# Sorted experts: the first products of a group in two PSUM buffers, tile by tile in turn, instead of in the two banks of one

## The chip, the cores and the metric

The kernel runs on one core of one Trainium2 chip. The metric is the device time in microseconds (us). Engines are named as in the profile: PE is TensorE's matmuls and PEld its weight loads, DVE is VectorE, ACT is ScalarE, POOL is GpSimd, SP is SyncE. PSUM is the memory that matmuls write; its banks hold 512 fp32 values per partition.

## What is computed

The reference is a stack of blocks on 2048 tokens of 128 features (linear layers, attentions, feed-forward layers, experts). The part that the change touches is the last step of the block `L3_ffn`, which occurs twice in the stack, once before and once after the attention `L3_attn`. Every token picks its two best of eight experts by a gate; the larger of the two numbers is the expert that it is sent to. That expert is a product to 256 features, a normalization, a GELU and a product back to 128:

```
chosen = jnp.max(top_i, axis=-1)
def expert(W1, B1, G, Bt, W2, B2, rsc):
    hh = xr @ W1 + B1
    hh = jax.nn.gelu(_ln(hh, G, Bt), approximate=False)
    return (hh @ W2 + B2) * rsc + xr
...
outs = jax.vmap(expert)(w1, b1, ln_g, ln_b, w2, b2, res_scale)
sel = jnp.take_along_axis(outs.transpose(1, 0, 2), chosen[:, None, None], axis=1)[:, 0]
moe = sel * jnp.sum(wts, axis=-1, keepdims=True)
```

## The kernel before

The stages follow one another: layers 0, 1 and 2, then the attention of the gated block, its experts, the attention `rope3`, the second gated attention, and its experts again. The change lies in `Experts.run` (line 1363), which therefore runs twice.

The experts are sorted. `route` gives each token a place in a list of tiles of 128 tokens that all have the same expert; there are eight first tiles, one for each expert, and up to fifteen extra ones for experts with more than 128 tokens, 23 tiles in all whatever the routing. `run` first works out which token lies in which slot (`who`, line 1421). Then it takes the 23 tiles in groups of four, the last of three, so six groups. Each group goes through four functions:

- `turned(b)`, line 1440: for each tile, an indirect DMA of POOL's queue gathers 128 rows of tokens (`xt`, line 1451, a ring of 4 buffers), for an extra tile another one loads that expert's weights (`wt`, line 1458, a ring of 11 buffers), and PE transposes the rows into one PSUM bank (`g_tp`). ACT copies the group's four transposes to SBUF (`gT`, line 1464) and writes the expert's selector (`sel`, line 1443).
- `first_product(b)`, line 1467: for each tile, PE adds the bias by a 16-row matmul (`ph<-b_b1s,sel`) and the product by `wt` (`ph<-wt,gT`, two instructions) in a PSUM region of 128 x 256; DVE takes its statistics (`st`, `mv`). After the last tile, DVE makes the reciprocal roots (`rs`, eleven short instructions) and normalizes tile by tile out of PSUM into SBUF (`hn`).
- `turned_back(b)`, line 1487: PE transposes each `hn` in two halves (`h_tp`), ACT takes the GELU of each (`hT`, line 1498).
- `second_product(b)`, line 1503: per tile a bias matmul and four instructions by `wt` into one bank (`po`); DVE copies the group's result to SBUF (`og_s`), SP sends it to DRAM.

The loop at line 1523 sets the order: `turned(b + 1)`, `turned_back(b)`, `first_product(b + 1)`, `second_product(b)`. With `order["pinned"]` set, PE's matmuls and transposes keep exactly this order. The other engines' instructions in this stage are not pinned; the framework places them, and sets every semaphore. When all groups are done, indirect DMAs gather the results back to the tokens (`yg`, line 1538), and `tail(c)` adds them to `x`, followed by what comes behind the experts: `rope3.prepare(c)` in the first run, `store(c)` in the second.

PSUM is shared out in pools (lines 1659 to 1661): `tp`, three buffers of one bank; `sc`, two buffers of two banks (`[P, 2, CW]`, 512 values each); `av`, one buffer of one bank. In this stage `bank(...)` takes a buffer of `tp`, `banks("ph")` a whole one of `sc`, and `out_bank` the one of `av`. In attention the score tiles `sn` take buffers of `sc` in turn (line 1027): PE writes one while DVE reduces the other. In `first_product`, one buffer of `sc` holds all four tiles of a group: tiles 0 and 1 in its first bank, 2 and 3 in its second.

Of the kernel before, what the change touches and what calls it, by code (L numbers as in the profile page):

```python
# [43 lines left out]
def tile_macaron(ctx: ExitStack, tc: tile.TileContext, a: dict, out: bass.AP):  # L44
# [30 lines left out]
    def mm(dst, lhsT, rhs, start=True, stop=True):  # L75
        pin(nc.tensor.matmul(dst, lhsT=lhsT, rhs=rhs, start=start, stop=stop))  # L76
# [98 lines left out]
    def inv_sqrt(pool, var, shape, tag, on_pool=False):  # L175
        v = pool.tile(shape, F32, tag=tag + "_v", name=tag + "_v")
        vec.tensor_scalar_add(v, var, 1e-5)
        g = pool.tile(shape, I32, tag=tag + "_g", name=tag + "_g")
        vec.tensor_scalar(g, v.bitcast(I32), -0.5, float(0x5F3759DF), ALU.mult, ALU.add)
        r = pool.tile(shape, F32, tag=tag + "_r", name=tag + "_r")  # L180
        prev = g.bitcast(F32)
        for _ in range(3):
            h = pool.tile(shape, F32, tag=tag + "_h", name=tag + "_h")
            if on_pool:
                nc.gpsimd.tensor_tensor(h, prev, prev, ALU.mult)
                nc.gpsimd.tensor_tensor(h, h, v, ALU.mult)
                nc.gpsimd.tensor_scalar(h, h, -0.5, 1.5, ALU.mult, ALU.add)
                nc.gpsimd.tensor_tensor(r, h, prev, ALU.mult)
            else:
                vec.tensor_tensor(h, prev, prev, ALU.mult)  # L190
                vec.scalar_tensor_tensor(h, h, -0.5, v, ALU.mult, ALU.mult)
                vec.scalar_tensor_tensor(r, h, 1.5, prev, ALU.add, ALU.mult)
            prev = r
        return r
# [477 lines left out]
    def ring(name, tag="w", shape=(P, CW), bufs=10):  # L672
        pool = pools["keep" if tag == "xnT" else "ring"]
        return pool.tile(list(shape), F32, tag=tag, name=name, bufs=bufs)
# [11 lines left out]
    def banks(name):  # L686
        if order["mode"] in ("host", "fill"):
            return TwoBanks(name)
        return pools["sc"].tile([P, 2, CW], F32, tag="sc", name=name)
# [6 lines left out]
    def out_bank(name):  # L696
        return pools["av"].tile([P, CW], F32, tag="av", name=name)
# [582 lines left out]
    class Experts:  # L1280
        F = 256
# [81 lines left out]
        def run(self, carried, after):  # L1363
# [8 lines left out]
            F, FB, NX = self.F, self.FB, self.NX  # L1372
# [44 lines left out]
            ps = out_bank("who_ps")[:, 0:NX]  # L1417
# [49 lines left out]
            def first_product(b):  # L1467
                s0, n = groups[b]
                g = made[b]
                mv = sb.tile([P, TC, 2], F32, tag="mv", name="mv", bufs=2)  # L1470
                ps = banks("ph")
                ph = [ps[:, k // 2, k % 2 * F : (k % 2 + 1) * F] for k in range(n)]
                for k in range(n):
                    mm(ph[k], g["sel"][:, k, :], b_1, stop=False)
                    mm(ph[k], g["gT"][:, k * P : (k + 1) * P], g["wts"][k][:, 0:F], start=False)
                    st = sb.tile([P, 6], F32, tag="st", name="st", bufs=2)
                    vec.bn_stats(st, ph[k])
                    vec.bn_aggr(mv[:, k, :], st)
                rs = inv_sqrt(sb, mv[:, :n, 1], [P, n], "rs")
                pair = [ring("hn") for _ in range(2)]  # L1480
                g["hn"] = [pair[k // 2][:, k % 2 * F : (k % 2 + 1) * F] for k in range(n)]
                for k in range(n):
                    vec.tensor_scalar(
                        g["hn"][k], ph[k], mv[:, k, 0:1], rs[:, k : k + 1], ALU.subtract, ALU.mult
                    )
# [34 lines left out]
            order["pinned"] = True  # L1520
            turned(0)
            first_product(0)
            for b in range(len(groups)):
                more = b + 1 < len(groups)
                if more:
                    turned(b + 1)
                turned_back(b)
                if more:
                    first_product(b + 1)
                second_product(b)  # L1530
# [259 lines left out]
```

## Time and profile before

| what | us |
|---|---|
| median of 3 runs (4014.67 to 4025.18) | 4024.48 |
| the profiled execution | 4027.38 |
| its span, first to last instruction | 4025.6 |
| expert stage, first run: first `ph` to last `og_s` | 2375.69 to 2468.32 |
| expert stage, second run | 3894.43 to 3987.21 |
| PE busy in 2365 to 2470 (105 us), granted clock 0.58 | 83.9 |
| DVE, ACT, POOL busy in the same stretch | 40.3, 23.8, 33.2 |

The profile shows one execution, with times in us from the start of the span. A line of the timeline gives the start, the length, the engine, the line of the kernel, the operation with what it writes and reads, the number of instructions, and in brackets how long the engine had been idle before and what released it. A line of a helper stands for all that call it: 76 is every matmul by `mm`, 84 every instruction of DVE, 94 every transpose. Matmuls overlap in the pipeline, so the distance from one start to the next tells more than the length of one. PEclk is the TensorE clock that was granted, 1.00 or 0.50 at any moment.

### The profile page before, as it was taken

The page shows a single profiled execution, that of the slowest core. Times are in us where ns is not written, and L with a number is a line of the kernel's source. Part 1 is how long each engine was busy: PE and PEld are TensorE (multiplying, and loading weights), DVE is VectorE, ACT ScalarE, POOL GpSimd, SP SyncE. Part 2 cuts the span into 40 slices and gives each one's busy share as a digit, 9 for nine tenths or more (in the row PEclk, how much of TensorE's full clock was granted, in tenths as well). Part 3 has the DMA queues.
Part 4 walks back from the last instruction along what each step waited for, and adds up shares of the span by engine and source line. Part 5 has one row for each costly group of instructions (what it writes and reads, how often), then busy time and mean ns, then how long its engine had stood idle before and what let it go on. Part 6 is the DMA issues. An engine that isn't in the chain of part 4 may idle for free. (4 is left out here: it accounts for less than half of the span.)

```text
span 4025.6 us, 72321 instructions
## 1 busy us (share of the span) xinstructions
PE 3590.0 (89%) x29144; PEld 1707.2 (42%) x29144; DVE 3117.3 (77%) x5468; ACT 2396.2 (60%) x4556; POOL 293.3 (7%) x473
## 2 busy tenths in 40 slices
PE   8789899699999999999999966688989899999965
PEld 8556655333333333333333333334333433333333
DVE  2855344689898986799999844689998799999844
ACT  1222133268686877688888722255767688888732
POOL 2000012220000000000000023200000000000013
PEclk8889789889999999799999965678899899999965
DMA  2100001111000000000000022310000000000012
GB/s 69 27 1 1 1 6 37 46 36 33 12 20 10 13 25 22 14 28 10 7 10 5 7 59 71 97 54 15 10 25 26 17 28 9 9 7 7 7 50 67
DMA packets 66063, 100.55 MB, mean 25 GB/s; under 512 B 10800, under 2 KB 31008, under 8 KB 65472
## 3 DMA queue, kind: packets, MB, share of 16 engines
q1 hardware_dynamic: 55184, 70.41, 5.8%
q0 software_dynamic: 9200, 24.94, 2.4%
q8 instruction: 230, 3.77, 0.4%
q14 instruction: 105, 0.86, 0.1%
q10 hardware_dynamic: 1344, 0.57, 0.1%
HBM read 65.29 MB, written 29.52 MB: 24 GB/s over the span
## 5 line engine op out<-in xcount | busy, mean ns | idle before, releaser
L84 DVE TENSOR_REDUCE h_mx<-sn 128x2 f32<-128x1024 f32 (+1 forms) x1856 | 2202.2, 1197 | 142.6 <-PE sn L1030 120.9
L1087 ACT ACTIVATE pr<-st 128x512 f32<-128x512 f32 x3712 | 1972.3, 585 | 486.2 <-PE st L76 319.6
L76 PE MATMUL av<-pr,va 128*32 128x256 f32 x14592 | 1193.6, 399 | 10.8 <-ACT h_ot L1116 10.2
L76 PE MATMUL st<-qp,kp 64*128 64x512 f32 x3712 | 1012.6, 501 | 34.7 <-ACT pr L1087 31.7
L1030 PE MATMUL sn<-kp,qp 64*128 64x512 f32 (+3 forms) x3712 | 826.3, 418 | 82.4 <-DVE h_mx L84 66.9
L76 PEld LDWEIGHTS st<-qp,kp 64*128 64x128 f32 x3712 | 401.9, 188 | 822.3 <-ACT pr L1087 448.4
L76 PEld LDWEIGHTS av<-pr,va 128*32 128x32 f32 x14592 | 294.3, 109 | 666.9 <-issue 626.0
L1030 PEld LDWEIGHTS sn<-kp,qp 64*128 64x128 f32 x3712 | 395.1, 196 | 132.7 <-DVE h_mx L84 80.9
L614 ACT ACTIVATE hid<-h 128x512 f32<-128x512 f32 x128 | 76.3, 597 | 235.3 <-PE h L76 229.7
L84 DVE TENSOR_TENSOR hid<-hid,h 128x512 f32<-128x512 f32 x128 | 87.4, 687 | 114.2 <-PE h L76 102.2
L76 PEld LDWEIGHTS po<-w_l_w3T,hid 128*128 128x128 f32 x1024 | 126.1, 193 | 39.0 <-issue 28.0
L76 PE MATMUL po<-w_l_w3T,hid 128*128 128x128 f32 x1024 | 127.7, 277 | 5.5 <-DVE hid L84 5.5
L76 PE MATMUL h<-m_xc,w_l_w12T 128*128 128x512 f32 x256 | 127.9, 638 | 0.0
L1458 POOL DMA_INDIRECT wt<-in_b_wt,w_row_i x30 | 28.7, 958 | 1245.2 <-DVE slot_i L84 1199.5
L76 PE MATMUL h<-xnT,w_l_w12T 128*128 128x512 f32 x256 | 117.4, 601 | 0.4 <-DVE logits L594 0.4
L84 DVE BATCH_NORM_STATS2 st<-ph 128x6 f32<-128x256 f32 x46 | 19.9, 432 | 90.3 <-PE ph L76 65.4
L247 POOL TENSOR_TENSOR x<-x,w_b_n2b 128x512 f32<-128x512 f32 x8 | 10.2, 1270 | 1064.0 <-ACT rows L213 1064.0
L1059 ACT CAST h_mT<-mt_ps 8x512 fp32r<-8x512 f32 x64 | 36.9, 576 | 75.9 <-PE mt_ps L94 75.6
L94 PE MATMUL xn_tp<-ident,xn_t 128*128 128x128 f32 x64 | 20.0, 390 | 63.5 <-ACT xn_t L213 52.7
L84 DVE TENSOR_TENSOR st<-st,mask_kq 128x128 f32<-128x128 f32 x256 | 63.4, 291 | 16.9 <-PE st L76 16.2
L76 PEld LDWEIGHTS h<-m_xc,w_l_w12T 128*128 128x128 f32 x256 | 49.9, 205 | 50.8 <-issue 48.1
L213 ACT ACTIVATE xn_t<-x,ln_nb,ln_r 128x128 f32<-128x128 f32 x64 | 26.4, 481 | 69.9 <-DVE ln_nb L84 49.1
(421 smaller groups left out, 2910.2 us busy)
## 6 DMA issues: line engine op xcount, KB each, us to landing
qp<-dq SPq DMA_DIRECT2D x128, 136.0 KB
kp<-dk SPq DMA_DIRECT2D x162, 64.0 KB
dq<-hi SPq DMA_DIRECT2D x32, 256.0 KB
dq<-lo SPq DMA_DIRECT2D x32, 256.0 KB
wt<-in_b_wt SPq DMA_DIRECT2D x16, 258.0 KB
qp<-h_mT SPq DMA_DIRECT2D x240, 4.0 KB
cos<-in_l_cos POOLq DMA_DIRECT2D x12, 256.0 KB
sin<-in_l_sin POOLq DMA_DIRECT2D x12, 256.0 KB
```

The source lines that it names most:

```text
L76: pin(nc.tensor.matmul(dst, lhsT=lhsT, rhs=rhs, start=start, stop=stop))
L84: ins = method(*args, **kw)
L94: pin(nc.tensor.transpose(dst, src, ident))
L213: nc.scalar.activation(dst[:, t, :], src[:, t, :], AF.Identity, bias=nb[:, t : t + 1], scale=rstd[:, t : t + 1])
L247: nc.gpsimd.tensor_tensor(xs, xs, row.unsqueeze(1).to_broadcast([P, TC, D]), ALU.add)
L614: nc.scalar.activation(hid[:, hb, :], p_1, AF.Silu)
L1030: pin(nc.tensor.matmul(sc[:, j, :wd], lhsT=qp[r, p, t * P : (t + 1) * P], rhs=kp[r, 2 * g + p, kc * CW : kc * CW + wd], start=True, stop=True,
L1059: nc.scalar.copy(mT, pt)
L1087: nc.scalar.activation(pr[:, off:CW], sc[:, off:], AF.Exp, scale=A.scale)
L1458: nc.gpsimd.indirect_dma_start(wts[k], None, a["b3_wt"], bass.IndirectOffsetOnAxis(ap=w_row_i[:, s - E : s - E + 1], axis=0),)
```

## The change

Where a group took one two-bank buffer of the pool `sc`, it now takes both. Of each it uses the first bank alone: tiles 0 and 2 lie in the two halves of the first buffer's bank, tiles 1 and 3 in those of the second. The matmuls, the statistics and the normalization are the same instructions in the same program order, on other addresses.

```diff
                 mv = sb.tile([P, TC, 2], F32, tag="mv", name="mv", bufs=2)
-                ps = banks("ph")
-                ph = [ps[:, k // 2, k % 2 * F : (k % 2 + 1) * F] for k in range(n)]
+
+                ps = [banks("ph") for _ in range(2)]
+                ph = [ps[k % 2][:, 0, k // 2 * F : (k // 2 + 1) * F] for k in range(n)]
                 for k in range(n):
                     mm(ph[k], g["sel"][:, k, :], b_1, stop=False)
                     mm(ph[k], g["gT"][:, k * P : (k + 1) * P], g["wts"][k][:, 0:F], start=False)
```

## The prediction

> **What bounds the kernel now.** I read the page first (shares, the clock line, the costliest groups), then the chain that ended last inside the expert stage, then the timelines of PE, DVE and POOL there, then the granted clock in stretches of 3.41 us.
>
> ```profile
> PEclk8889789889999999799999965678899899999965
> ...
> L84 DVE BATCH_NORM_STATS2 st<-ph 128x6 f32<-128x256 f32 x46 | 19.9, 432 | 90.3 <-PE ph L76 65.4
> ```
>
> The change touches only the expert stage, which runs twice: from the first `ph` to the last `og_s` copy, 2375.69 to 2468.32 (92.6 us) and 3894.43 to 3987.21 (92.8 us). The clock line sags there to 0.6 and 0.5. The statistics of the first products, 46 of 0.43 us, wait for PE each time. The chain in the first run, columns start, length, what:
>
> ```profile
> 2377.69 0.44 DVE st L84
> 2378.18 1.74 PE ph L76 x3
> 2379.95 0.44 DVE st L84
> 2380.43 1.74 PE ph L76 x3
> 2382.20 0.44 DVE st L84
> ```
>
> PE and DVE take turns: three matmuls of a tile, its statistics, the next tile. The timeline of PE says the same of every tile but the first of a group, of the third as well, which lies in the other bank. So the wait hangs on the whole two-bank buffer, not on the bank. At half clock:
>
> ```profile
> 2380.94 1.22 PE L76 MATMUL ph<-wt,gT 128*128 128x256 f32 x2
> 2382.69 0.58 PE L76 MATMUL ph<-b_b1s,sel 16*128 16x256 f32 x1 [0.52 <-DVE st L84]
> 2383.20 1.22 PE L76 MATMUL ph<-wt,gT 128*128 128x256 f32 x2
> 2384.21 1.06 PE L94 MATMUL g_tp<-ident,xt 128*128 128x128 f32 x4
> ```
>
> and at full clock:
>
> ```profile
> 2409.67 0.38 PE L76 MATMUL ph<-b_b1s,sel 16*128 16x256 f32 x1 [0.53 <-DVE st L84]
> 2409.97 0.70 PE L76 MATMUL ph<-wt,gT 128*128 128x256 f32 x2
> 2410.71 0.43 DVE L84 BATCH_NORM_STATS2 st<-ph 128x6 f32<-128x256 f32 x1 [0.88 <-issue]
> ...
> 2411.20 0.38 PE L76 MATMUL ph<-b_b1s,sel 16*128 16x256 f32 x1 [0.53 <-DVE st L84]
> ...
> 2411.51 0.70 PE L76 MATMUL ph<-wt,gT 128*128 128x256 f32 x2
> ...
> 2412.14 0.32 PE L76 MATMUL po<-b_b2s,sel 16*128 16x128 f32 x1
> ```
>
> **What goes: the waits.** Half clock: tile to tile is 2.25 us (2380.43 to 2382.69). Unwaited, the bias matmul takes 0.51 (2382.69 to 2383.20) and the pair 1.01 (2383.20 to 2384.21, where the next work starts): 1.52. A wait costs 0.73. Full clock: 1.53 against 0.31 + 0.63 = 0.94, so 0.59. After the change tile 1 has a buffer of its own, and tile 2 shares one with tile 0, whose statistics started 0.74 after its pair (2409.97 to 2410.71) and are done 0.48 later, at 1.22; tile 2 comes 0.63 + 0.94 = 1.57 after that pair. It is covered by tile 1, with 0.35 to spare at full clock; without that cover two waits a group come back. Groups of 4, 4, 4, 4, 4 and 3 tiles have 17 waits a run; counting pitches in the timelines, 10 at half and 7 at full clock in either run. Sum: 20 x 0.73 + 14 x 0.59 = 14.6 + 8.3 = **22.9 us**.
>
> **What the two buffers cost.** Formerly a group took one buffer and left the other to its neighbour. Now it takes both, so the next group needs them back. But PE's order is fixed, and the transposes `h_tp` of a group, which need all its `hn`, the last reader of the buffers, stand ahead of the next group's `ph`. That wait is paid already: 0. No instruction and no DMA is added. On ACT, eight GELUs (2406.64 to 2409.54) lie under the next `ph`; four unwaited tiles at full clock last 3.8 us from 2406.59, still 0.8 more. On DVE a tile's two statistics need 0.65, under 0.94.
>
> **What is moved: the clock.** The granted clock steps in stretches of 3.41 us (PE busy with its instructions, then the clock):
>
> ```profile
> core 0: us, PE busy (x), PEclk, DMA share, GB/s
> 2399.15:2402.56 3.41, 3.41 (x13) 0.50 0.19 29
> 2402.56:2405.98 3.42, 3.42 (x16) 0.50 0.62 194
> 2405.98:2409.39 3.41, 2.64 (x12) 1.00 0.49 135
> 2409.39:2412.80 3.41, 2.61 (x10) 1.00 0.37 105
> 2412.80:2416.22 3.42, 3.42 (x13) 0.50 0.29 75
> ```
>
> A dense stretch with transposes lifts it, and then the waited `ph` tiles leave PE 2.4 to 2.7 us of work in a stretch, and it falls back, so `po` runs at half. Sorting the whole trace's stretches so: of 805 at full clock with 2.8 us or more of work, 799 were followed by full clock; with 2.2 to 2.8 only 38 of 57; and at half clock none with under 3.0 us was ever lifted. Without waits `ph` and `po` leave PE full, so I expect the clock to hold once it is up. At full clock a group is 4 x 0.94 = 3.8 (`ph`), 4 x 0.98 = 3.9 (`po`, 3930.97 to 3931.95), and transposes of 0.9 and 0.5 (1.71 and 0.85 at half, less 0.40 for each four: 0.66 for four at 2330.24 at full clock against 1.06): 9.1 us.
>
> Then POOL is late next. Its queue issues four row and four weight gathers in a group:
>
> ```profile
> 2405.12 0.95 POOL L1451 DMA_INDIRECT xt<-xg,who  x1 [0.82 <-PE g_tp L94]
> ...
> 2406.38 0.95 POOL L1451 DMA_INDIRECT xt<-xg,who  x1 [0.30 <-issue]
> ```
>
> 8 x 1.25 = 10.0 us, so the three groups with weight gathers cost 10.0 each, not 9.1. A run then is: to the first `h_tp`, 12.4 less 3 x 0.73: 10.2; to the second, 17.2 less 2.2: 15.0, still at half clock; three groups at 10.0: 30.0; `h_tp`, three `ph`, four `po` at full clock: 7.6; the last group, whose `hn` (4.3 us behind its last statistics) now outlasts `po` by 0.5: 0.5 + 1.2 + 2.9 + 0.7 = 5.3. Together 68.1 against 92.6: 24.5 a run. If the clock rises a group earlier, lifted by bare `ph` (no row shows such a stretch), `ph` and `po` give 4.6 more, 29 a run; if a row gather, which lands 3.9 us after its issue (2371.39 to 2375.28), is 1 us later in each cycle, 3 less. I take 25, **50 us** for both. The profiled execution took 4027.4 (span 4025.6 and 1.8 around it), which gives 3977; the median shown is 2.9 lower: 4024.5 - 50 = 3974.5, rounded to **3975**.
>
> A rule that speaks against this last part: the Trainium skill, "TensorE: Matmul & The Clock Gate", section "Part 4: PE-mode transpose", says that transposes do not count as PE work for the clock. The trace disagrees: the stretch at 2399.15, `po` alone and full, was not followed by full clock, while the one at 2402.56, with transposes of rows and of `hn` in it, was. The same page, section "HAM oscillation — how this bites in real kernels", tells of PSUM double-buffering that gave no further gain in a kernel whose loop had been put in order: by it the sum would be 0. Here the wait that goes stands in the chain itself.
>
> **Rivals.**
> - *Only the waits go.* The clock goes on falling, since POOL's late rows leave gaps in each group; 10 of the 42 full-clock stretches with 2.4 to 2.8 us of work were followed by half clock. Then 22.9: 4001.6. For it: the fall at 2412.80 came after a stretch with 2.61. Against it: `po` after a dense `ph` has no gap before the next gathers. If the page's rule on transposes held, this is also what would come out.
> - *The waits stay*, because two buffers of the pool are tracked as one: 4024. Against it: attention's score tiles `sn` lie in the same pool, and DVE reduces one (1.20 us each, 2202 us busy with 143 idle before them) while PE writes the next.
> - *Slower, by POOL's queue.* Only PE's order is pinned; POOL's is chosen anew. If the fourth row gather lands behind the next group's weight gathers, which wait for `po` (issues at 2413.54, 2415.09 and 2416.64), it goes out at about 2417.9 instead of 2410.14. Its transpose then waits 5.2 to 6.5 us (a 1.25 issue or two and 3.9 to land behind the last `po`) in three cycles of each run: 31 to 39 us, less 22.9: up to 4040. It decides from 3.8 us a cycle (22.9 / 6) on. For it: one weight gather stands between row gathers today. Against it: nothing in the diff reaches POOL.
>
> **How the numbers follow.** Clock holds, 3962 to 3987: 0.62. Waits alone or a clock that holds in part, 3987 to 4012: 0.23. More than 62 us (full clock from the first group on): 0.04. Within 0.3% (12 us, about what a measurement of this kernel can tell from no change): 0.06, the waits that stay and part gains eaten by POOL. Slower by more: 0.05. The range runs from the early rise (58 us, and some drift of attention's clock: the three runs lie 10.5 us apart) to the waits alone and a little less: 3962 to 4005, which leaves out about 0.2.
>
> **What would show it.** The changed kernel should have no `ph` waiting for `st`; tile pitches of 1.52 and 0.94; clock 1.00 from the second `h_tp` of a run to its last `po`; the stage 92.6 down to 65 to 70 us; `g_tp` waiting for `xt` from the third group on. I am wrong if the clock still alternates (about 4002), if `ph` waits elsewhere, or if rows are later than 4 us a cycle.

## The result, and the profile after

| what | before, us | after, us |
|---|---|---|
| median of 4 runs each | 4023.93 (4014.67 to 4025.18) | 3968.77 (3968.13 to 3970.36) |
| the profiled execution, its span | 4027.38, 4025.6 | 3968.13, 3966.3 |
| expert stage, first run | 92.62 | 66.49 (2374.26 to 2440.77) |
| expert stage, second run | 92.78 | 66.23 |
| time at half clock in the two runs of the stage | 75.6, 75.7 | 27.5, 26.8 |
| all that lies between the two runs of the stage | 1426.1 | 1422.4 |

The ratio is 0.987 (95%: 0.9856 to 0.9884): 55 us less. The two stages give 26.1 and 26.5, together 52.7. The rest lies ahead of, between and behind them, where nothing was changed and where executions differ by a few us anyway.

The clock line of the page of after; the two runs of the stage (slices 24 and 25, and the last two) now show 0.7, where they showed 0.6 and 0.5. The single 5 lies behind the first run:

```profile
PEclk8889789879999999799999977578989899999977
```

The view of the tile `st` in the stage's first run, for the kernel after (what it waited for, who waited for it, each with us and times):

```profile
its engine sat idle before it (us, times) until:
  PE ph L76: 27.1, 23
who waited for it (us, times):
  PEld ph L76: 2.3, 7
```

All 23 statistics still wait for their product. The other direction is gone: in the same view of before, PE's matmuls waited for `st` 13 times by name (6.8 us) and its weight loads as often (14.0); here only seven weight loads do, 2.3 us in all, under matmuls that are still running. The chain of waits, first run, after:

```profile
2386.79 6.64 PE ph L76 x12
2393.43 6.21 PE po L76 x20
...
2402.03 3.76 PE ph L76 x12
2405.78 3.58 PE po L76 x20
```

Where PE and DVE took turns, twelve `ph` now stand in one piece, followed by twenty `po`. PE's timeline, after, at half clock and then at full clock:

```profile
2376.15 0.58 PE L76 MATMUL ph<-b_b1s,sel 16*128 16x256 f32 x1
2376.66 1.22 PE L76 MATMUL ph<-wt,gT 128*128 128x256 f32 x2
2377.81 0.58 PE L76 MATMUL ph<-b_b1s,sel 16*128 16x256 f32 x1
...
2402.90 0.38 PE L76 MATMUL ph<-b_b1s,sel 16*128 16x256 f32 x1
2403.20 0.70 PE L76 MATMUL ph<-wt,gT 128*128 128x256 f32 x2
2403.84 0.38 PE L76 MATMUL ph<-b_b1s,sel 16*128 16x256 f32 x1
```

No bracket, so no idle time; the pitch is 1.66 (2376.15 to 2377.81) and 0.94 (2402.90 to 2403.84). The granted clock in stretches of 3.41 us, after (columns: PE, PEld, DVE, ACT and POOL busy with instructions, then the clock, the DMA share and GB/s):

```profile
2391.46:2394.87 3.41, 3.41 (x9) 2.00 (x8) 1.84 (x8) 0.00 (x0) 0.00 (x0) 0.50 0.00 0
2394.87:2398.29 3.42, 3.42 (x12) 2.69 (x11) 3.07 (x12) 0.00 (x0) 1.89 (x2) 0.50 0.27 77
2398.29:2401.70 3.41, 3.41 (x16) 3.29 (x17) 0.69 (x1) 1.21 (x2) 2.22 (x3) 0.50 0.66 185
2401.70:2405.12 3.42, 3.42 (x14) 1.74 (x12) 1.46 (x5) 2.90 (x8) 2.53 (x3) 1.00 0.36 104
2405.12:2408.53 3.41, 3.41 (x19) 2.50 (x18) 2.70 (x14) 0.00 (x0) 2.22 (x3) 1.00 0.35 102
```

The clock comes up behind the stretch that holds `po`, `g_tp` and `h_tp`, as before the change, but now stays up for 41.0 us, to the end of the stage.

### The profile page after: what moved, and what is told of

Its sections match the earlier page's. It is cut to its first block, busy times and chain, and to the rows that moved or that the text cites. A ratio compares the mean times of both kernels' runs of the same rounds, so it can differ in the third digit from the quotient of the medians.

```text
span 3966.3 us, 72318 instructions
## 1 busy us (share of the span) xinstructions
PE 3554.6 (90%) x29144; PEld 1676.7 (42%) x29144; DVE 3114.6 (79%) x5468; ACT 2395.2 (60%) x4556; POOL 292.9 (7%) x473
## 5 line engine op out<-in xcount | busy, mean ns | idle before, releaser
L247 POOL TENSOR_TENSOR x<-x,w_b_n2b 128x512 f32<-128x512 f32 x8 | 10.2, 1272 | 1059.1 <-ACT rows L213 967.4
L84 DVE TENSOR_TENSOR st<-st,mask_kq 128x128 f32<-128x128 f32 x256 | 63.4, 290 | 18.4 <-PE st L76 17.1
L76 PEld LDWEIGHTS h<-xnT,w_l_w12T 128*128 128x128 f32 x256 | 46.9, 194 | 47.2 <-issue 46.0
```

The costliest lines, as they stand in the source:

```text
L84: ins = method(*args, **kw)
L247: nc.gpsimd.tensor_tensor(xs, xs, row.unsqueeze(1).to_broadcast([P, TC, D]), ALU.add)
```

## The experiments

The theory: the wait hangs on the whole buffer; with two buffers the waits go, PE stays full, and the clock holds once it is up. Rivals: what counts is the bank; only the waits count and the clock is a side effect; the first group's pace and not that of each group brings the clock; POOL's queue sets the pace behind it. The runs were made in three sets, each on a chip of its own, with the kernel before run on the same chip (4024.67, 4027.66 and 4031.23); ratios are to it.

**One buffer, tiles in its two banks in turn** (on the kernel before):

```diff
-                ph = [ps[:, k // 2, k % 2 * F : (k % 2 + 1) * F] for k in range(n)]
+                ph = [ps[:, k % 2, k // 2 * F : (k // 2 + 1) * F] for k in range(n)]
```

> One two-bank buffer as before, but the tiles take its two banks in turn (0 and 2 in the first bank, 1 and 3 in the second). If the wait hangs on the whole buffer, every ph tile but a group's first still waits for the statistics of the one ahead: 4024 us, give or take 6. If it hangs on the bank, this does all that the change does: 3969 us.

Measured: 4025.4, ratio 1.0007 (0.9994 to 1.002). Its trace has all 17 waits in each run of the stage, 0.52 to 0.53 us each, as before. Taking turns between banks does nothing; the wait is on the buffer.

**Two buffers, but tiles 0 and 1 in the first and 2 and 3 in the second**:

```diff
-                ph = [ps[k % 2][:, 0, k // 2 * F : (k // 2 + 1) * F] for k in range(n)]
+                ph = [ps[k // 2][:, 0, k % 2 * F : (k % 2 + 1) * F] for k in range(n)]
```

> Two buffers, but tiles 0 and 1 in the first and 2 and 3 in the second: 11 of the 17 waits of a run stay (behind tiles 0 and 2 of a group), 6 go. Waits alone are worth 0.6 us each, 12 x 0.6 = 7: 4017 us. If a gain comes in proportion to the waits gone, 55 x 12 / 34 = 19: 4004 us. If a group with two waits still keeps the clock at full speed, the loss against the change is 22 x 0.6 = 13: 3982 us.

Measured: 3988.3, ratio 0.9912 (0.9895 to 0.9929). With 22 of the 34 waits still there, most of the gain is there too: the stage was 81.3 (51.6 at half clock) in the first run and 73.3 (30.5) in the second. Twelve waits are some 7 us, so most of the 36 us came by the clock, which held in part: in the first run it fell in some of the groups and was lifted again a group later, while in the second it held for 44.4 us with 11 waits in the run.

**The waits kept, their gaps filled** (on the kernel before): a 16-row bias matmul into a buffer that nothing reads, behind each tile but the last. It adds work and takes no wait away.

```diff
+                spare = banks("spare")
                 ps = banks("ph")
...
+                    if k + 1 < n:
+                        mm(spare[:, 0, 0:F], g["sel"][:, k, :], b_1)
```

> The kernel before with one more bias matmul of 16 x 256 behind each tile but a group's last, into a buffer that nothing reads: all 34 waits stay, but PE has work in them. If full PE work holds the clock, the stage runs at full clock from the second h_tp on and only the waits themselves are lost against the change, 34 x 0.6 = 20: about 3990 us. If the gain were the waits alone, this is no faster than before: 4024 us or more.

Measured: 4019.86, ratio 0.9986 (0.9971 to 1.0001); stage 95.1 and 92.8, with 81.4 and 75.8 at half clock. The expectation fell. At full clock the gap behind a tile shrank from 0.53 to 0.21, and yet in the first run the clock fell after each lifted stretch. Such a stretch of this kernel (the columns as above):

```profile
2401.13:2404.55 3.42, 2.99 (x12) 1.49 (x10) 1.20 (x4) 2.90 (x8) 2.51 (x4) 1.00 0.39 105
```

PE was busy for 2.99 of 3.42 us, which by the sorting in the prediction should have held the clock. The next stretch was at half.

**The same with all rows in use**: the filler is a 128 x 128 x 128 product.

```diff
+                    if k + 1 < n:
+                        mm(spare[:, 0, 0:P], ident, ident)
```

> The kernel before with a 128 x 128 x 128 fp32 matmul (two instructions, 0.36 us at full clock) behind each tile but a group's last, in place of the 16-row one: all 34 waits stay, and PE's gap is about the same 0.2 us as with the 16-row one. If what the clock counts is work on all rows of the array, this holds it where 16 rows did not: 66.5 + 7 at most per stage, about 3990 us, with 30 us at half clock per run in place of 76. If any waiting gap drops it, whatever PE does beside: 4020 us as with 16 rows, with 76 to 81.

Measured: 4011.88, ratio 0.9974 (0.9962 to 0.9986); stage 84.9 and 85.0, with 44.1 and 47.6 at half clock. The second stretch after its lift:

```profile
2403.63:2407.05 3.42, 2.90 (x13) 2.00 (x13) 1.55 (x6) 0.11 (x1) 1.28 (x2) 1.00 0.37 100
```

It is no busier than the one above, and its gaps are wider (0.30 against 0.21), yet the clock stayed for 17.1 us, until two statistics came 2.1 us late (told of below). So busy time alone doesn't tell; 128-row work held the clock where 16-row work of about the same length did not. And with every tile still at the pitch of before (2.25 at half clock, 1.53 at full), the higher clock alone took some 8 us off each run of the stage. That is a gain by the clock without a gain by the waits.

**Only the first group in two buffers**, and, with `b == 0` in place of `b > 0`, **only the first group in one buffer** (both written as an edit to the changed kernel):

```diff
-                ps = [banks("ph") for _ in range(2)]
-                ph = [ps[k % 2][:, 0, k // 2 * F : (k // 2 + 1) * F] for k in range(n)]
+                if b > 0:
+                    ps = banks("ph")
+                    ph = [ps[:, k // 2, k % 2 * F : (k % 2 + 1) * F] for k in range(n)]
+                else:
+                    ps = [banks("ph") for _ in range(2)]
+                    ph = [ps[k % 2][:, 0, k // 2 * F : (k // 2 + 1) * F] for k in range(n)]
```

> The kernel before with only the first group's products of a run in two buffers: 3 of the 17 waits of a run go, all in the first group; 14 stay. If the pace of every later group is what holds the clock, the stage is 92.7 - 1.8 = 90.9 us, a few us less if one more stretch is lifted, and the time 4010 to 4021. If one fast group is enough to lift the clock and it then holds by itself, the stage is 66.4 + 14 x 0.6 = 74.8 us and the time 3986.

Measured: 4024.08, ratio 0.9984 (0.9971 to 0.9997); stage 93.3 and 91.0. The clock was lifted four times in the first run, each time for a single stretch:

```profile
2408.51:2411.92 3.41, 2.29 (x7) 0.96 (x6) 1.26 (x5) 1.54 (x5) 2.04 (x3) 1.00 0.37 97
```

One fast group brings nothing that lasts: the clock has to be held by the later groups. That each of them must be free of waits is not shown, since the clock held for 44.4 us with 11 waits in one run of the kernel with pairs.

> The changed kernel with the first group's products of a run in one buffer as before: 3 of the 17 waits of a run come back, all in the first group, at half clock (0.60 us each). If the clock is lifted by the stretch of second products and transposes behind the first group and not by the first group's own pace, the stage is 66.4 + 1.8 = 68.2 us and the time 3972.4. If the first group's pace is what brings the lift, the second group runs at half clock too (15 us instead of 9) and the time is about 3984 or more.

Measured: 3994.24, ratio 0.9905 (0.9888 to 0.9921), beside 3989.8 for the changed kernel itself in the same set (below). The clock came up at the same place as in the changed kernel, at the start of the third group's `ph` (at 2404.6, with `ph` from 2403.29; after the change at 2401.7, with `ph` from 2401.96). 4.4 us more than the control is near the 3.6 of six waits, and far from 15. But the four runs of the control alone lie 26 us apart, since statistics came late here too (by up to 5.3 us, told of below), so the time decides little; the place of the lift is the firmer evidence.

**The pace of POOL**: one more small gather for each extra tile, 12 issues in a group instead of 8 (on the changed kernel).

```diff
+            again = [small_tile([P, 8], f"again{k}") for k in range(2)]
...
+                    if s >= E:
+                        nc.gpsimd.indirect_dma_start(
+                            again[k % 2], None, xg[:, :].rearrange("s (a b) -> (s a) b", b=8), bass.IndirectOffsetOnAxis(ap=who[:, s : s + 1], axis=0)
+                        )
```

> The changed kernel with one more gather of POOL's queue (128 rows of 32 bytes, into tiles that nothing reads) behind each extra tile's row gather: twelve issues a group, 15.0 us, in place of eight, 10.0, against 9.1 us that PE needs. If POOL is just short of the bound now, the three groups with weight gathers take up to 15 us each: 3 x 5.9 less some 3 us of head start, 15 a run, and the clock falls in the gaps: 4000 us or more. If POOL has room to spare: 3969 us.

Measured: 4010.86, ratio 0.9962 (0.9946 to 0.9979); stage 82.6 and 83.5, 16 and 17 us above after, and some 8 above the two other variants of the changed kernel on this chip (73.4 to 75.3, below). This is not the plain answer that it seems: in the first run PE waited for a row gather inside the groups once, for 0.52 us. The largest single loss of the run is another one, in the second group (PE, ACT and DVE lines of the timeline; `hT` is a GELU of ACT that waits for `h_tp`):

```profile
2388.18 1.22 PE L76 MATMUL ph<-wt,gT 128*128 128x256 f32 x2
...
2389.79 0.46 ACT L1504 ACTIVATE hT<-h_tp,wt 128x128 f32<-128x128 f32 x1 [4.87 <-PE ph L76]
...
2398.21 0.43 DVE L84 BATCH_NORM_STATS2 st<-ph 128x6 f32<-128x256 f32 x1 [11.22 <-remote]
2398.70 0.58 PE L76 MATMUL ph<-b_b1s,sel 16*128 16x256 f32 x1 [7.64 <-DVE st L84]
2398.78 0.40 DVE L84 BATCH_NORM_STATS2 st<-ph 128x6 f32<-128x256 f32 x1
```

By the records, the product of tile 0 was done at 2389.40 and DVE began its statistics 8.8 us later, having nothing else to do. The second run has the same delay (8.9 us) at the same tile. DVE was not the only one: ACT's first GELU began 2.05 us behind the recorded end of the last `h_tp` (2387.74), where in after it begins 0.18 ahead of that end. And the statistics of tile 1 began only 0.57 us behind those of tile 0, though by the pitch its product ends 1.66 behind. So tile 0's product must have been finished at least 1.1 us (an estimate from these rows) before DVE was let go: that much of the delay, at the least, lay in the signal from PE and not in its work. The run shows that this kernel with more gathers is a good deal slower, but not that POOL's issues do it by being late with rows.

**PE warmed ahead of the first group**: three 128 x 512 products that nothing reads, before the first transposes (on the changed kernel).

```diff
             order["pinned"] = True
+            warm = out_bank("warm")
+            for _ in range(3):
+                mm(warm, ident, x[:, 0:TC, :].rearrange("p t d -> p (t d)"))
```

> The changed kernel with three dense fp32 matmuls of 128 x 512 (six instructions, 5 us at half clock) ahead of each run's first transposes, while PE waits for the gathers. If a dense stretch lifts the clock and it then holds, the first two groups run at full clock too: 2 x 2.9 (ph) + 2.6 (po) + 0.5 (h_tp) = 9 a run, 3951 us. If it is lifted but falls again in the 3.3 us before the first h_tp, at most the first ph gains, 2.9 a run: 3963 us. If the gathers' gaps drop it at once: 3969 us.

Measured: 3964.31, ratio 0.9848 (0.9832 to 0.9865); stage 66.5 and 67.0, no shorter than after. The products took 4.99 us and lifted the clock, but the next stretch had only 1.58 us of work between the first row gathers, and the clock was at half again when `ph` began.

**PE warmed in every gap of the first groups** (on the changed kernel):

```diff
+                    if b == 0 and k + 1 < n:
+                        stoke(F)
...
+            warm = out_bank("warm")
+
+            def stoke(cols):
+                mm(warm[:, 0:cols], ident, self.place[0][:, 0:cols])
+
+            for _ in range(3):
+                stoke(CW)
             turned(0)
...
+                if b == 0:
+                    for _ in range(3):
+                        stoke(CW)
                 turned_back(b)
```

> The changed kernel with dense fp32 matmuls in all of PE's gaps at a run's start: three of 512 columns ahead of the first transposes, one of 256 between each two of them, three of 512 ahead of the first h_tp. If full PE work lifts and holds the clock, the first two groups run at full clock: 9 us a run less, a little given back where a filler delays a transpose (up to 1): 3953 us, half-clock time in the stage near 0 in place of 27. If the clock falls all the same: 3969 to 3975 us.

Measured: 3989.67, ratio 0.9914 (0.9895 to 0.9933); stage 73.4 and 73.5. The first groups did run at full clock (`ph` at a pitch of 0.94 from 2375.56 on, where after has 1.66), but late statistics as in the kernel with more gathers, of up to 5.4 us, took the clock away in the third group and once more in the fifth. Inconclusive on what a warm start is worth.

**All four banks of the two buffers** (on the changed kernel):

```diff
-                ph = [ps[k % 2][:, 0, k // 2 * F : (k // 2 + 1) * F] for k in range(n)]
+                ph = [ps[k % 2][:, k // 2, 0:F] for k in range(n)]
```

> The changed kernel with both banks of each buffer in use, a bank for each of a group's four tiles. If the second pair's wait is fully covered by the tile between, as reckoned (0.35 us to spare at full clock), nothing changes: 3969 us. If tiles that share a bank still hold each other up, it is faster, by up to 22 waits of 0.6: 3956 us.

Measured: 3992.81, ratio 0.9915 (0.9894 to 0.9936); stage 74.9 and 75.3, 24 us above after. So it was run again, beside the changed kernel itself:

> The four-banks kernel once more: each of the two buffers holds its two tiles in two banks instead of one. If two tiles in one bank and two tiles in two banks are alike (the wait is on the buffer), it is within 0.3% of the control beside it. If the banks matter, it is 24 us above the control, as it was above the changed kernel before.

> The changed kernel itself once more, beside the next three on one chip. If the longer stage of the four-banks kernel came from its banks, this one is at 3969 (66.4 us from the first product to the last output copy of a run). If it came from the conditions of that batch, this one is near 3990 too, with a DVE or PE instruction of the stage that starts some 3 us late without a releaser among the kernel's own work.

Measured: 3983.67 for four banks, ratio 0.9886 (0.9858 to 0.9913); 3989.8 for the changed kernel, ratio 0.9892 (0.986 to 0.9925), with stages of 71.8 and 74.2. The banks make no difference that these runs show. The changed kernel itself took some 21 us more in that set than in the first measurement, and its trace shows where: the clock, up at 2401.8, fell at 2415.4 in the first run. PE and DVE lines of the timeline of the repeated run of the changed kernel, fourth group:

```profile
2411.56 0.70 PE L76 MATMUL ph<-wt,gT 128*128 128x256 f32 x2
2412.50 0.70 PE L76 MATMUL ph<-wt,gT 128*128 128x256 f32 x2
2413.71 0.43 DVE L84 BATCH_NORM_STATS2 st<-ph 128x6 f32<-128x256 f32 x1 [2.29 <-PE ph L76]
2414.20 0.38 PE L76 MATMUL ph<-b_b1s,sel 16*128 16x256 f32 x1 [1.00 <-issue]
```

Tile 0's product is recorded as done at 2412.26; its statistics started at 2413.71, 1.45 us later, and only then could tile 2 start, which shares that buffer. PE idled 1.00 us, then 0.48 at the next tile. The stretch from 2412.02 to 2415.43 had 2.19 us of work, and three stretches at half clock followed.

## Why the prediction was right, step by step

- *The wait is on the buffer, and goes.* Right: one buffer with banks in turn changed nothing (4025.4), and after the change no `ph` of PE waits for `st`. Tile 2 was covered as worked out, in the runs where the statistics come on time. Of the changed kernel's two traces, the first has all 46 of them start within 0.5 us of the recorded end of their product.
- *What a wait costs.* 0.59 at full clock stood. At half clock the unwaited pitch is 1.66, not 1.52. The pair had been sized at 1.01 by the start of what follows it in before, a transpose; ahead of the next bias matmul it is 1.15. So a wait was worth 0.60 (2.26, from 2380.43 to 2382.69, less 1.66), not 0.73, and the sum is 20 x 0.60 + 14 x 0.59 = 20.3 us, not 22.9.
- *The two buffers cost nothing.* Right: `h_tp` of the group ahead had already waited for the buffers' last reader. In the chain of after, `ph` follows `h_tp` at once in every group (2402.03 behind 2400.50 + 1.53). Nor did POOL's queue change its order, as the rival "slower" had it: one weight gather stands between the third row gather and the fourth, before (2408.88) and after (2403.88).
- *The clock holds from the second `h_tp` on.* Right, and it is the larger part: 52.7 less 20.3 leaves 32.4 us, with 48 and 49 us less at half clock in the two runs. The two halves were seen apart: a higher clock without fewer waits in the 128-row filler (some 8 us a run), and, in the kernel with only its first group in two buffers, three missing waits a run without the clock (7 us less in all than the kernel before beside it). The reason given was too simple: 2.8 us of busy PE in a stretch was not enough when the filler used 16 rows.
- *POOL is late next, 10.0 us a group.* Mis-sized. From `h_tp` to `h_tp`, the two groups that run wholly at full clock took 9.12 and 9.02 (2409.64 to 2418.76, and to 2427.78). POOL does issue every 1.25 us, without a pause from 2406.95 to 2424.51, but it was ahead when the fast groups began, and it loses only 0.9 us a group. After three of them it is about level: the second run's chain has it once,

```profile
3911.81 4.77 DMA xt<-xg,who
```

and the first run's has none. "`g_tp` waiting for `xt` from the third group on" was thus wrong but for one place.
- *PE's own 9.1 us a group.* The sum came out by two misses that cancel. `po` took 3.58 a group, not 3.9: its tile of 0.98 was read from 3930.97 to 3931.95, and there the clock fell at 3931.73; a tile wholly at full clock takes 0.89 (2405.72 to 2406.61). The eight `h_tp` took 1.35 (2409.80 to 2411.15), not 0.9, since their pairs come at the pace of DVE's `hn` (four in 1.90 us from 2408.76).
- *The sum of the stage*, first run:

| term | predicted | measured |
|---|---|---|
| to the first `h_tp` | 10.2 | 10.6 |
| to the second `h_tp` | 15.0 | 15.5 |
| three groups | 30.0 | 27.5 |
| `h_tp`, three `ph`, four `po` | 7.6 | 8.0 |
| the last group | 5.3 | 5.0 |
| together | 68.1 | 66.5 |

The two terms at half clock are short by the 0.14 a tile of the pitch; the three groups were 2.5 too long by POOL. A gain of 26 a run where 24.5 was worked out and 25 taken. The misses have opposite signs, so that 50 lies this near to 55 is in part luck, as are the conditions: in the third set the gain was some 41 (4031.23 to 3989.8).
- *What the Trainium skill tells.* The clock again came up behind a stretch in which transposes have a large part (2398.29), not behind the two full ones ahead of it. That agrees with the row the prediction drew on, and not with the rule of the Trainium skill, "TensorE: Matmul & The Clock Gate", section "Part 4: PE-mode transpose", that transposes do not count. That a second PSUM buffer brings nothing more, as the same page's section "HAM oscillation — how this bites in real kernels" tells of one kernel, was not so here: the time fell by 1.3%.
- *What the prediction had not thought of:* that the clock, once up, can be lost when one engine's start behind another comes late. In the third set, on a chip of its own, the same kernel took 3976.6 to 4003.1, ratio 0.9892 (0.986 to 0.9925). It was still clearly faster than before.

What stays open is what makes the statistics late. Delays of over 0.5 us are in none of the traces of before and after, nor in the four kernels of the first set (46 of 46 on time in each). In the other two sets they are in seven of the eight traces, in 4 to 12 tiles each, up to 8.9 us. The eighth is the kernel with only its first group in two buffers, which is nearly as slow as before. The longest delay is in the one with more gathers. That could point to gathers that come close together, on some chips, but no run shows it: the kernel before has no trace in those sets, and the chip of the first measurement is not on record. The matmuls' ends are modelled, so PE's records alone don't tell whether its work was late or its signal; the one place that tells is the second group of the kernel with more gathers, where at least 1.1 us lay in the signal. What held it is open.

## What to carry to other kernels

Where one engine writes a tile that another reads and both take turns, look at what the wait hangs on: here it was the whole two-bank buffer, and spreading tiles over its banks was worth nothing, while tiles in turn over two buffers took the wait away with the same memory. Price such a wait by the clock too: here 20 us of waits came with 32 us more that the half clock cost. A gain by the clock is also easily lost: four statistics that began 1.3 to 2.0 us late went with a run of the stage that was 5 us longer (71.8 against 66.5). A queue that was a little too slow for the new pace (10.0 us a group against 9.1) held PE up in one place only, since it started ahead and the stage is short.

## What the runs showed of the hardware

- The time that PE is busy did not decide alone whether the clock holds: 2.99 of 3.42 us with 16-row fillers was followed by half clock, 2.90 with 128-row ones by full clock.
- A stretch full by the records need not lift the clock from half: after `ph` and `po` with 3.41 of 3.41 us (2391.46 and 2394.87) it stayed at 0.50, each with bias matmuls of 16 rows in it. 4.99 us of 128-row products lifted it (2369.50 in the warmed kernel).
- DVE began a tile up to 8.9 us behind the recorded end of its product in some executions, at the same tile in both runs of one kernel, with DVE idle before it. ACT was late behind the transposes just ahead (2.05 us), and the next tile's statistics followed by 0.57 us, so part of the delay lay between PE and its readers.
